# Expert products with w2 by one level of Strassen's algorithm in a graph and attention layer on one Trainium2 core

## The chip, the cores and the metric

The kernel runs on one core of one Trainium2 chip. The metric is the device time of one launch in microseconds; the kernel before takes 1625.79 us, the median of three runs (1625.36 to 1625.93). The profile is of one execution, whose span from the first to the last instruction is 1623.3 us.

## The reference

N = 4096 tokens of C = 256 channels pass a graph layer (a dense 4096x4096 adjacency times the features), causal attention with four heads, and a mixture of eight experts of which each token uses two. All arithmetic is fp32. The change is in the last part:

```python
flat = _rmsnorm(x, ln2_w).reshape(-1, Cx)
probs = jax.nn.softmax(flat @ router_w.T, axis=-1)
tp, ti = jax.lax.top_k(probs, TOPK)
...
for e in range(NE):
    hh = jax.nn.silu(flat @ w1[e].T) * (flat @ w3[e].T)
    out = out + weights[:, e:e + 1] * (hh @ w2[e].T)
return x + out.reshape(Bx, Tx, Cx)
```

The hidden size of an expert is 682: five chunks of 128 and a tail of 42.

## The kernel before

The program runs in three stages on the one core: the graph layer (to about 539 us), attention (its scores end at 1092 us) and the experts (hidden products from 1099 us to the end, the last steps of attention and routing among the first five turns). Instructions stand on each engine in the order in which the code emits them, so the order of the Python calls is the order of every engine's queue.

**Token groups.** For each expert, the routing stage has written the rows of its tokens (256 channels, the token's number, eight gate weights) into a list in DRAM. A group is 256 tokens of one expert (a whole group, two halves of 128) or 128 tokens (a small group). 42 groups are worked off in turns k = 0 to 41; the list `TURNS` gives the group of a turn. Turns 0 to 8 are whole groups; from 9 on whole and small ones mostly alternate (small at 9, 11, 13, 15, 16, 18, 20, 22, 24, 25, 27, 29, 31, 32, 34, 36 and 38), and turns 39, 40 and 41 are whole. 25 turns are whole and 17 small.

**A turn.** The loop over k emits: `hidden(k)`; the load of w1 and w3 for turn k + 3; `combine(k - 1)`; the load of the rows of turn k + 4; the load of w2 for turn k + 2. So the second products of a turn come after the first products of the next.

- `hidden(k)` (lines 1095 to 1126): for q = 0, 2, 4 a PSUM tile of two banks gets up to four 128-row blocks of w1 and w3 times the tokens (L1106); ScalarE takes silu of the w1 half (L1112); VectorE multiplies it with the w3 half into hT (L1113). The tail of 42 rows goes through L1121 and L1123 into a tile of its own. There are three such PSUM tiles in turn, two buffers for silu's output, and two each of hT and tail. After the first q the tokens of turn k + 1 are turned by TensorE (`prepare`, L1084: four 128x128 transposes for a whole group, two for a small one) in PSUM bank y, and two ScalarE operations (L1089) bring them into SBUF as xT.
- `combine(k)` (lines 1128 to 1178): VectorE picks the tokens' gate weights (pick L1135, gt L1139). For each half of 128 tokens six products of 256 columns (five chunks and the tail, L1151) accumulate in bank y. VectorE scales the sum by gt into y (L1162), and GpSimd adds y to the tokens' rows in DRAM by an indirect DMA (L1167, the put). The puts go to `acc_dram` up to turn 38. Then `acc_dram` is copied to `out` (L1268), and the puts of turns 39, 40 and 41 go to `out`. Turns 40 and 41 use bank ms for the first half and bank y for the second.

Banks y and ms are single buffers of 2 KB per partition. Weights lie in three rotating places cut out of two large tiles that earlier stages used (qT_all, res_all), so a product's name shows one of those as its source. All weight and row loads go through SyncE's one queue.

The graph stage already uses one level of Strassen's algorithm: lines 375 to 378 make sums of the adjacency, 400 to 403 those of the features, and lines 444 to 451 put seven products together.

Of the kernel before, what the change touches and what calls it, by code (L numbers as in the profile page):

```python
# [9 lines left out]
F32 = mybir.dt.float32  # L10
I32 = mybir.dt.int32
SP = mybir.EngineType.SP
AF = mybir.ActivationFunctionType
ALU = mybir.AluOpType
# [3 lines left out]
P = 128  # L18
N = 4096
C = 256  # L20
# [6 lines left out]
NF = 5  # L27
TAIL = HID - NF * P
T0 = 64
# [12 lines left out]
GR = 256  # L42
SM = 128
NA = -((NE * (GR - 1) - 2 * (N - 512)) // GR)
NW = -((NE * (GR - 1) - 2 * N) // GR)
# [8 lines left out]
NM = NG - RARE  # L54
# [12 lines left out]
def fast_kernel(  # L67
# [24 lines left out]
    nc = tc.nc  # L92
# [85 lines left out]
    kT = [kvp.tile([P, 512], F32, name=f"kT{b}") for b in range(NB)]  # L178
# [38 lines left out]
    with (  # L217
# [82 lines left out]
        T3 = G12  # L300
        HC = C // 2
# [230 lines left out]
    with (  # L532
# [259 lines left out]
                join(put, "late writes")  # L792


        def after(b):

            return [
                [None, lambda: inputs(b)],
                [None],
                [lambda: project(b, 0)],  # L800
                [lambda: project(b, 1)],
                [lambda: turn(b, 0)],
                [lambda: turn(b, 1), lambda: residual(b)],
                [lambda: logits(b)],
                [lambda: weigh(b)],
                [None, lambda: choose(b)],
                [None, lambda: scaled(b, 0)],
                [None, lambda: scaled(b, 1)],
                [lambda: place(b), lambda: scaled(b, 2)],
                [None, lambda: scaled(b, 3), lambda: scatter(b, 0, 0)],  # L810
                [None, lambda: scatter(b, 0, 1), lambda: scatter(b, 1, 0)],
                [None, lambda: scatter(b, 1, 1), lambda: scatter(b, 2, 0)],
                [None, lambda: scatter(b, 2, 1), lambda: scatter(b, 3, 0)],
                [None, lambda: scatter(b, 3, 1)],
            ]


        def last_qkv():
            b, made = NB - 1, {}

            def scales():
                stats(ax, b)
                var = mv[b][:, :, 1:2]
                power(rstd[b], var, 1.0, EPS_LN)
                power(both[b], var, *BOTH)

            def norm():
                made["h0"] = ax.tile([P, TB, ROW], F32, tag="row", name="h0_l")
                for t in range(TB):
                    normed(made["h0"][:, t, 0:C], b, t, both[b][:, t])  # L830

                made["hT"] = qT[b]

            def turned(h):
                tr = p_ms.tile([P, 2, 2, P], F32, tag="ms", name=f"tr_l{h}")
                for t in range(2):
                    for c in range(2):
                        nc.tensor.transpose(
                            tr[:, c, t, :], made["h0"][:, 2 * h + t, c * P : (c + 1) * P], ident
                        )  # L840
                for c in range(2):
                    nc.scalar.activation(
                        made["hT"][:, c, h * 2 * P : (h + 1) * 2 * P],
                        tr[:, c].rearrange("p t i -> p (t i)"),
                        AF.Copy, scale=ln1_sb[:, c : c + 1],
                    )

            def rotate(t):
                pj = p_ms.tile([P, 512], F32, tag="ms", name=f"pq_l{t}")
                room = ex.tile([P, NF, GR], F32, tag="hT", name=f"ro_l{t}")  # L850
                ro, r2 = (
                    room.rearrange("p k i -> p (k i)")[:, k : k + 384].rearrange(
                        "p (h s d) -> p h s d", s=2, d=HD // 2
                    )
                    for k in (0, 384)
                )
                rotated(ax, b, t, made["hT"], pj, ro, r2, cos_l[:, t, None, :], sin_l[:, t, None, :])
                made[t] = ro

            def turn_heads(t):  # L860
                tr = p_ms.tile([P, 2, 2, P], F32, tag="ms", name=f"trq_l{t}")
                heads(b, t, made.pop(t), tr)

            return [
                [None, scales], [None, norm], [lambda: turned(0)], [lambda: turned(1)],
                [lambda: rotate(0)], [lambda: rotate(1)],
                [lambda: turn_heads(0)], [lambda: rotate(2)],
                [lambda: turn_heads(1)], [lambda: rotate(3)],
                [lambda: turn_heads(2)], [lambda: turn_heads(3)],
                *guard(),  # L870
            ]
# [157 lines left out]
                join(put, "pads")  # L1029


        tails = [eg.tile([P, GR], F32, name=f"tail{n}") for n in range(2)]
        for t in tails:
            nc.gpsimd.memset(t, 0.0)

        at13 = (qT_all[:, 0 : 2 * W13], qT_all[:, 2 * W13 : 4 * W13], res_all[:, 0 : 2 * W13])
        W2 = (NF + 1) * C
        at2 = (
# [39 lines left out]
        def prepare(k, pool=p_y, tag="y"):  # L1078
# [13 lines left out]
                )  # L1092
            inputs_of[i] = xT

        def hidden(k, step=None, behind=None):
            i = TURNS[k]
            n = halves(i) * P
            w13_sb, xT = w13s[k % 3], inputs_of.pop(i)
            hT = ex.tile([P, NF, n], F32, tag="hT", name=f"hT_{i}")

            for q in range(0, NF + 1, 2):
                ps = next(p_sc).tile([P, 2, 2, GR], F32, tag="sc", name=f"h_{i}_{q}")
                ps = ps[:, :, :, 0:n]
                for m in range(2 * q, min(2 * q + 4, 2 * NF + 1)):
                    for c in range(2):
                        nc.tensor.matmul(  # L1106
                            ps[:, m % 2, m // 2 - q, :], w13_sb[:, c, m * P : (m + 1) * P],
                            xT[:, c, :], start=(c == 0), stop=(c == 1),
                        )
                both = 2 if q + 1 < NF else 1  # L1110
                si = ax.tile([P, 2, n], F32, tag="rden", name=f"si_{i}_{q}")
                nc.scalar.activation(si[:, 0:both, :], ps[:, 0, 0:both, :], AF.Silu)  # L1112
                nc.vector.tensor_mul(  # L1113
                    hT[:, q : q + both, :], si[:, 0:both, :], ps[:, 1, 0:both, :]
                )
                if q == 0 and behind is not None:
                    prepare(behind)
                if step and q < NF - 1:
                    step()

            nc.scalar.activation(si[T0 : T0 + TAIL, 1, :], ps[0:TAIL, 0, 1, :], AF.Silu)  # L1121
            tail = tails[k % 2][:, 0:n]
            nc.vector.tensor_mul(  # L1123
                tail[T0 : T0 + TAIL, :], si[T0 : T0 + TAIL, 1, :], ps[T0 : T0 + TAIL, 0, 1, :]
            )
            hidden_of[i] = (hT, tail)

        def combine(k):
            i = TURNS[k]
            n = halves(i)  # L1130
            w2_sb = w2s[k % 3]
            hT, tail = hidden_of.pop(i)
            r = rows.pop(i)
            pick = ex.tile([P, n, NE], F32, tag="pick", name=f"pick_{i}")
            nc.vector.tensor_mul(  # L1135
# [4 lines left out]
            y = ax.tile([P, HALF, C], F32, tag="yT1", name=f"y_{i}")  # L1140

            last = k >= NM - 2
            ps = [
                pool.tile([P, HALF, C], F32, tag=tag, name=f"ye_{i}_{tag}")
                for pool, tag in ((p_ms, "ms"), (p_y, "y"))[0 if last else 1 :]
            ]

            def products(h):
                cols = slice(h * P, (h + 1) * P)
                for q in range(NF + 1):  # L1150
                    nc.tensor.matmul(  # L1151
                        ps[h if last else 0][:, h, :],
                        hT[:, q, cols] if q < NF else tail[:, cols],
                        w2_sb[:, q, :], start=(q == 0), stop=(q == NF),
                    )

            for h in range(0 if last else n):
                products(h)
            for h in range(n):
                if last:  # L1160
                    products(h)
                nc.vector.tensor_scalar(  # L1162
                    y[:, h, :], ps[h if last else 0][:, h, :], gt[:, h], None, op0=ALU.mult
                )
                at = bass.IndirectOffsetOnAxis(ap=r[:, h, C : C + 1].bitcast(I32), axis=0)
                nc.gpsimd.memset(gap, 0.0)
                put = nc.gpsimd.indirect_dma_start(  # L1167
                    out=(acc_dram if k < NM - LAST else out)[:, :],
                    out_offset=at,
                    in_=y[:, h, :], in_offset=None, compute_op=ALU.add,  # L1170
                )
                if h:
                    free(put, f"half {i}", "an expert has a token once")
                else:
                    join(put, f"half {i}")
                if i < NA:
                    free(put, "last x", "the tokens of the first groups are others")
                    join(put, "first sums")
# [834 lines left out]
```

## Time and profile before

| what | from | value |
|---|---|---|
| median time | times | 1625.79 us |
| span of the profiled execution | page | 1623.3 us |
| granted TensorE clock, mean | cores | 0.998 |
| products with w2 in bank y (L1151) | tile | 780 records in 65 halves |
| transposes of tokens (L1084) | tile | 134 |
| hidden products (L1106) | page | 1848 records, 335 us busy |
| y scaled (L1162), 128x256 | page | 65, 481 ns each |
| puts to acc_dram and out (L1167) | page and groups | 67, 1.57 us of GpSimd each |
| w1 and w3 of a turn | DMA issues | 1408 KB, 7.6 to 8.0 us to landing |
| w2 of a turn | DMA issues | 768 KB, 5.0 to 5.3 us to landing |

How to read it: PE is TensorE's matmuls, PEld its weight loads, DVE is VectorE, ACT ScalarE, POOL GpSimd, SP SyncE. A timeline line gives the start, the duration, the engine, the code line, the operation, its output and inputs, the shape and how many instructions are merged; in brackets is the idle time before it and what ended it. Durations of matmuls overlap, as they are pipelined, so the distance of their starts is what one costs in a stream. A group's line gives total busy time and the mean of one in ns, then the idle time before.

### The profile page before, as it was taken

The numbers are of one execution on the slowest core, as the hardware profiler recorded it, in microseconds if no ns is written. First come the engines' busy times: TensorE is split into PE (matmuls) and PEld (weight loads), VectorE is DVE, ScalarE is ACT, GpSimd is POOL, SyncE is SP. The second block draws the span as 40 slices with busy tenths as digits, with TensorE's granted clock in tenths as the row PEclk, the third lists the DMA queues.
The fourth block names the chain that finished last, engine by engine and source line by source line (L and its number), as shares of the span: only waits on it lengthen the run. The fifth ranks groups of instructions, "written<-read, shape, count | busy, mean of one in ns | idle before, by whom it ended". The sixth has DMA issues, their size and how long they took to land.

```text
span 1623.3 us, 24752 instructions
## 1 busy us (share of the span) xinstructions
PE 1600.2 (99%) x9588; PEld 1156.7 (71%) x9588; DVE 930.4 (57%) x1914; ACT 457.1 (28%) x866; POOL 402.6 (25%) x604
## 2 busy tenths in 40 slices
PE   8999999999999999999999999999999999999997
PEld 5779999999999544343343433338888998999986
DVE  5656656656665678778878888793432222222222
ACT  2110100000000455554454554553211121221211
POOL 1001111112112220443334332322422222222122
PEclk9999999999999999999999999999999999999999
DMA  6224434433433000000101000067756777777765
GB/s 227 98 77 143 151 130 160 147 142 135 159 134 133 4 0 1 24 31 28 37 17 40 28 13 28 22 195 229 241 160 206 230 250 235 233 246 220 243 222 148
DMA packets 67711, 209.73 MB, mean 129 GB/s; under 512 B 14656, under 2 KB 46272, under 8 KB 53952
## 3 DMA queue, kind: packets, MB, share of 16 engines
q1 hardware_dynamic: 54592, 190.32, 33.7%
q0 software_dynamic: 12720, 17.47, 5.6%
q8 instruction: 78, 1.28, 0.3%
q14 instruction: 49, 0.40, 0.1%
q10 hardware_dynamic: 272, 0.26, 0.0%
HBM read 180.81 MB, written 31.42 MB: 131 GB/s over the span
## 4 chain that ended last, share of the span: by engine, by line
PE 91%; DVE 5%; ACT 2%; issue 1%; DMA 0%; POOL 0%; SPq 0%; DVEq 0%; POOLq 0%; ACTq 0%
PE acc L424 24%; PE h L1106 20%; PE ya L591 12%; PE sc L556 11%; PE ye_y L1151 10%; PE pf L386 3%; DVE sum L579 3%; PE pq L184 3%; PE po L625 2%; ACT pt L561 1%; PE tx L1084 1%; PE dn L604 1%; PE tr L319 1%; DVE rden L609 1%; PE trq L212 1%
## 5 line engine op out<-in xcount | busy, mean ns | idle before, releaser
L561 ACT ACTIVATE pt<-sc 128x1024 f32<-128x1024 f32 (+3 forms) x288 | 251.7, 958 | 201.4 <-PE sc L556 168.0
L579 DVE TENSOR_TENSOR sum<-sum,pt 128x1024 f32<-128x1024 f32 (+3 forms) x258 | 293.8, 1139 | 20.5 <-POOL pt L563 0.5
L424 PE MATMUL acc<-g,a 128*128 128x128 f32 x2048 | 255.7, 275 | 0.0
L556 PE MATMUL sc<-qT_all,kT 64*128 64x512 f32 (+3 forms) x1152 | 251.7, 570 | 3.0 <-ACT pt L561 2.2
L591 PE MATMUL ya<-pt,vv 128*64 128x512 f32 (+3 forms) x1152 | 242.6, 563 | 0.0
L424 PEld LDWEIGHTS acc<-g,a 128*128 128x128 f32 x2048 | 241.8, 192 | 0.0
L1106 PE MATMUL h<-xT,qT_all 128*128 128x256 f32 (+1 forms) x1232 | 220.5, 335 | 0.0
L1113 DVE TENSOR_TENSOR hT<-si,h 128x256 f32<-128x256 f32 (+2 forms) x126 | 64.1, 509 | 260.9 <-ACT si L1112 260.9
L1106 PEld LDWEIGHTS h<-xT,qT_all 128*128 128x128 f32 x1232 | 194.2, 191 | 18.9 <-issue 1.0
L556 PEld LDWEIGHTS sc<-qT_all,kT 64*128 64x128 f32 x1152 | 103.5, 186 | 138.8 <-issue 104.0
L591 PEld LDWEIGHTS ya<-pt,vv 128*64 128x64 f32 x1152 | 76.3, 136 | 145.4 <-issue 139.9
L1167 POOL DMA_INDIRECT acc_dram<-y,rows x61 | 96.1, 1575 | 332.2 <-DVE y L1162 327.8
L1112 ACT ACTIVATE si<-h 128x256 f32<-128x256 f32 (+2 forms) x126 | 57.2, 454 | 376.2 <-PE h L1106 371.0
L1106 PE MATMUL h<-xT,res_all 128*128 128x256 f32 (+1 forms) x616 | 114.6, 342 | 0.0
L1106 PEld LDWEIGHTS h<-xT,res_all 128*128 128x128 f32 x616 | 100.3, 191 | 10.2 <-issue 0.2
L424 PE MATMUL acc<-g,more_sums 128*128 128x129 f32 (+1 forms) x768 | 101.7, 275 | 0.6 <-DVE more_sums L377 0.6
L424 PEld LDWEIGHTS acc<-g,more_sums 128*128 128x128 f32 x768 | 94.6, 192 | 7.5 <-issue 7.5
L1151 PE MATMUL ye_y<-res_all,hT 128*128 128x256 f32 x430 | 99.8, 379 | 0.0
L783 POOL DMA_INDIRECT lists<-row,slots x64 | 69.0, 1077 | 114.8 <-issue 111.8
L1151 PEld LDWEIGHTS ye_y<-res_all,hT 128*128 128x128 f32 x430 | 80.9, 190 | 10.5
L1162 DVE TENSOR_SCALAR y<-ye_y,gt 128x256 f32<-128x256 f32 x65 | 29.3, 481 | 86.0 <-PE ye_y L1151 85.9
L424 PE MATMUL acc<-g,qT_all 128*128 128x128 f32 (+1 forms) x512 | 74.0, 274 | 0.0
(231 smaller groups left out, 1713.6 us busy)
## 6 DMA issues: line engine op xcount, KB each, us to landing
a<-in_adj_dram SPq DMA_DIRECT2D x64, 1024.0 KB, 4.7
qT_all<-in_w_dram SPq DMA_DIRECT2D x28, 1408.0 KB, 8.0
res_all<-in_w_dram SPq DMA_DIRECT2D x28, 768.0 KB, 5.3
res_all<-in_w_dram SPq DMA_DIRECT2D x14, 1408.0 KB, 7.6
qT_all<-in_w_dram SPq DMA_DIRECT2D x14, 768.0 KB, 5.0
rows<-lists SPq DMA_DIRECT2D x25, 265.0 KB, 2.8
lists<-pad SPq DMA_DIRECT2D x8, 662.5 KB, 13.9
res_all<-in_x_dram SPq DMA_DIRECT2D x8, 512.0 KB, 10.0
```

Source lines behind the costliest of these rows:

```text
L184: nc.tensor.matmul(pj, hT[:, c, t * P : (t + 1) * P], wqkv_sb[:, c, :], start=(c == 0), stop=(c == 1),)
L424: nc.tensor.matmul(acc[t][bank][:, at : at + w], m[left][:, k, t * P : (t + 1) * P], g[jb][:, right, k, 0:w], start=(jb == 0 and k == 0 an ...
L556: nc.tensor.matmul(ps[:, j, :w], kT[sb][hd, i * P : (i + 1) * P], qT[b][hd, p, off:], start=True, stop=True,)
L561: nc.scalar.activation(pt[:, :, :w], ps[:, :, :w], AF.Exp, scale=HD ** -0.5)
L579: nc.vector.tensor_add(sums[b, p][:, :, off:], before[:, :, off:], pt[:, :, : 512 - off])
L591: nc.tensor.matmul(accs[b, p][hd, off:], vv[sb][:, i, hd], pt[:, j, : 512 - off], start=(s == 0), stop=(s == TB * b + TB - 1),)
L783: put = nc.gpsimd.indirect_dma_start(out=lists[:, :], out_offset=bass.IndirectOffsetOnAxis(ap=chosen[b][:, k, t, :], axis=0), in_=flats[b] ...
L1106: nc.tensor.matmul(ps[:, m % 2, m // 2 - q, :], w13_sb[:, c, m * P : (m + 1) * P], xT[:, c, :], start=(c == 0), stop=(c == 1),)
L1112: nc.scalar.activation(si[:, 0:both, :], ps[:, 0, 0:both, :], AF.Silu)
L1113: nc.vector.tensor_mul(hT[:, q : q + both, :], si[:, 0:both, :], ps[:, 1, 0:both, :])
L1151: nc.tensor.matmul(ps[h if last else 0][:, h, :], hT[:, q, cols] if q < NF else tail[:, cols], w2_sb[:, q, :], start=(q == 0), stop=(q == NF),
L1167: put = nc.gpsimd.indirect_dma_start(out=(acc_dram if k < NM - LAST else out)[:, :], out_offset=at, in_=y[:, h, :], in_offset=None, comput ...
```

## The change

A product of a whole group is (256 tokens x 768) times (768 x 256), the 768 being five chunks, the tail and zeros around the tail. One level of Strassen's algorithm (in Winograd's form) cuts tokens, the inner dimension and the outputs in two each and makes seven products of halves in place of eight, at the price of sums before and after. It is done in 17 turns: 6, 7, 8, 10, 12, 14, 17, 19, 21, 23, 26, 28, 30, 33, 35, 37 and 39. It is for having fewer columns to stream through TensorE.

- The tail becomes the sixth chunk of hT, which is now two fixed tiles for even and odd turns. The rotation of the last block's heads borrows the same tiles.
- `split(k)` stands at the end of `hidden(k)`: eight VectorE operations of 128x384, four on the hidden values and four on w2. Sums go to buffers that attention has left (kT, vv), two sets for even and odd turns; S3 and T3 are written over their inputs.
- `seven_products(k)` stands in `combine(k)`: seven products of 128 columns, three chunks each; four in bank y and three in bank ms. Then one ScalarE copy and seven VectorE additions of 128x128 make the four quarters, and ScalarE scales the two halves into y in place of VectorE.
- From turn 6 on `prepare` of the next turn stands at the end of `hidden`, in bank ms, and no longer after the first q in bank y.

```diff
+        SEVEN = [k for k in range(6, NM - 2) if TURNS[k] < NW]
...
+            first = k % 2 * 3
+            for n, s in enumerate(("S1", "S2", "S4")):
+                m[s] = kT[first + n][:, 0 : 3 * P].rearrange("p (j i) -> p j i", j=3)
+            for n, s in enumerate(("T1", "T2", "T4")):
+                m[s] = vv[first + n][:, 0:3, :]
+            m["S3"], m["T3"] = m["A21"], m["G12"]
+            nc.vector.tensor_add(m["S1"], m["A21"], m["A22"])
+            nc.vector.tensor_sub(m["S2"], m["S1"], m["A11"])
+            nc.vector.tensor_sub(m["S4"], m["A12"], m["S2"])
+            nc.vector.tensor_sub(m["S3"], m["A11"], m["A21"])
+            nc.vector.tensor_sub(m["T1"], m["G12"], m["G11"])
+            nc.vector.tensor_sub(m["T3"], m["G22"], m["G12"])
+            nc.vector.tensor_sub(m["T2"], m["G22"], m["T1"])
+            nc.vector.tensor_sub(m["T4"], m["T2"], m["G21"])
...
+            for number, left, right in (
+                (1, "A11", "G11"), (2, "A12", "G21"), (6, "S2", "T2"), (7, "S3", "T3"),
+                (5, "S1", "T1"), (3, "S4", "G22"), (4, "A22", "T4"),
+            ):
+                n = len(p)
+                p[number] = banks[n // 4][:, n % 4, :]
+                for j in range(3):
+
+                    nc.tensor.matmul(
+                        p[number], m[left][:, j, :], m[right][:, j, :],
+                        start=(n % 4 == 0 and j == 0), stop=(j == 2), skip_group_check=True,
+                    )
...
+            nc.scalar.copy(u2, p[1])
+            nc.vector.tensor_add(c[0][:, 0], u2, p[2])
+            nc.vector.tensor_add(u2, u2, p[6])
+            nc.vector.tensor_add(u3, u2, p[7])
+            nc.vector.tensor_add(u4, u2, p[5])
+            nc.vector.tensor_add(c[0][:, 1], u4, p[3])
+            nc.vector.tensor_sub(c[1][:, 0], u3, p[4])
+            nc.vector.tensor_add(c[1][:, 1], u3, p[5])
...
-            hT = ex.tile([P, NF, n], F32, tag="hT", name=f"hT_{i}")
+            hT = hTs[k % 2][:, :, 0:n]
+            free_bank = k >= SEVEN[0]
...
-                if q == 0 and behind is not None:
+                if q == 0 and behind is not None and not free_bank:
                     prepare(behind)
...
+            if behind is not None and free_bank:
+                prepare(behind, p_ms, "ms")
+            hidden_of[i] = hT
+            if k in SEVEN:
+                split(k, hT)
...
+                if seven:
+                    nc.scalar.activation(
+                        y[:, h, :], done[h].rearrange("p h o -> p (h o)"), AF.Copy, scale=gt[:, h]
+                    )
+                else:
+                    nc.vector.tensor_scalar(
+                        y[:, h, :], ps[h if last else 0][:, h, :], gt[:, h], None, op0=ALU.mult
+                    )
```

More of the change, by code (lines that the diff above doesn't have):

```diff
@@ L792, in scatter @@
                 join(put, "late writes")
+        hTs = [eg.tile([P, NF + 1, GR], F32, name=f"hT{n}") for n in range(2)]
+        for t in hTs:
+            nc.gpsimd.memset(t[:, NF, :], 0.0)
         def after(b):
@@ L849, in rotate @@
                 pj = p_ms.tile([P, 512], F32, tag="ms", name=f"pq_l{t}")
-                room = ex.tile([P, NF, GR], F32, tag="hT", name=f"ro_l{t}")
+                room = hTs[t % 2]
                 ro, r2 = (
@@ L1029, in write_pads @@
                 join(put, "pads")
-        tails = [eg.tile([P, GR], F32, name=f"tail{n}") for n in range(2)]
-        for t in tails:
-            nc.gpsimd.memset(t, 0.0)
         at13 = (qT_all[:, 0 : 2 * W13], qT_all[:, 2 * W13 : 4 * W13], res_all[:, 0 : 2 * W13])
@@ L1093, in prepare, with split @@
             inputs_of[i] = xT
+        SEVEN = [k for k in range(6, NM - 2) if TURNS[k] < NW]
+        parts_of = {}
+        def split(k, hT):
+            w2_sb = w2s[k % 3]
+            m = {}
+            for c in range(2):
+                chunks = hT.rearrange("p (j c) i -> p c j i", c=2)[:, c]
+                weights = w2_sb.rearrange("p (j c) o -> p c j o", c=2)[:, c]
+                for h in range(2):
+                    m[f"A{h + 1}{c + 1}"] = chunks[:, :, h * P : (h + 1) * P]
+                    m[f"G{c + 1}{h + 1}"] = weights[:, :, h * P : (h + 1) * P]
+            first = k % 2 * 3
[12 more added lines that the diff above has]
+            nc.vector.tensor_sub(m["T4"], m["T2"], m["G21"])
+            parts_of[k] = m
@@ new lines, in seven_products @@
+        def seven_products(k):
+            i = TURNS[k]
+            m = parts_of.pop(k)
+            HC = C // 2
+            banks = [
+                pool.tile([P, 4, HC], F32, tag=tag, name=f"ye_{i}_{tag}")
+                for pool, tag in ((p_y, "y"), (p_ms, "ms"))
+            ]
+            p = {}
+            for number, left, right in (
[9 more added lines that the diff above has]
+                    )
+            c = [vv[6 + k % 2].rearrange("p (r h) o -> p r h o", r=2)[:, r] for r in range(2)]
+            u2 = u4 = c[0][:, 1]
+            u3 = c[1][:, 1]
+            nc.scalar.copy(u2, p[1])
[6 more added lines that the diff above has]
+            nc.vector.tensor_add(c[1][:, 1], u3, p[5])
+            return c
@@ L1121, in hidden @@
             nc.scalar.activation(si[T0 : T0 + TAIL, 1, :], ps[0:TAIL, 0, 1, :], AF.Silu)
-            tail = tails[k % 2][:, 0:n]
             nc.vector.tensor_mul(
-                tail[T0 : T0 + TAIL, :], si[T0 : T0 + TAIL, 1, :], ps[T0 : T0 + TAIL, 0, 1, :]
+                hT[T0 : T0 + TAIL, NF, :], si[T0 : T0 + TAIL, 1, :], ps[T0 : T0 + TAIL, 0, 1, :]
             )
-            hidden_of[i] = (hT, tail)
+            if behind is not None and free_bank:
[3 more added lines that the diff above has]
+                split(k, hT)
         def combine(k):
@@ L1131, in combine @@
             w2_sb = w2s[k % 3]
-            hT, tail = hidden_of.pop(i)
+            hT = hidden_of.pop(i)
             r = rows.pop(i)
@@ L1142, in combine @@
             last = k >= NM - 2
[L1143 to L1146, printed above, removed]
+            seven = k in SEVEN
+            if seven:
+                done = seven_products(k)
+            else:
+                ps = [
+                    pool.tile([P, HALF, C], F32, tag=tag, name=f"ye_{i}_{tag}")
+                    for pool, tag in ((p_ms, "ms"), (p_y, "y"))[0 if last else 1 :]
+                ]
             def products(h):
@@ L1152, in products @@
                         ps[h if last else 0][:, h, :],
-                        hT[:, q, cols] if q < NF else tail[:, cols],
-                        w2_sb[:, q, :], start=(q == 0), stop=(q == NF),
+                        hT[:, q, cols], w2_sb[:, q, :], start=(q == 0), stop=(q == NF),
                     )
-            for h in range(0 if last else n):
+            for h in range(0 if last or seven else n):
                 products(h)
@@ L1161, in combine @@
                     products(h)
-                nc.vector.tensor_scalar(
-                    y[:, h, :], ps[h if last else 0][:, h, :], gt[:, h], None, op0=ALU.mult
-                )
+                if seven:
+                    nc.scalar.activation(
+                        y[:, h, :], done[h].rearrange("p h o -> p (h o)"), AF.Copy, scale=gt[:, h]
+                    )
+                else:
+                    nc.vector.tensor_scalar(
+                        y[:, h, :], ps[h if last else 0][:, h, :], gt[:, h], None, op0=ALU.mult
+                    )
                 at = bass.IndirectOffsetOnAxis(ap=r[:, h, C : C + 1].bitcast(I32), axis=0)
```

## The prediction

> **What bounds the kernel now.** I read the page's busy shares first, then the table of stretches, then the timeline of one pair of expert turns, then the groups with shapes kept apart, then the timeline of the last 50 us.
>
> ```profile
> PE 1600.2 (99%) x9588; PEld 1156.7 (71%) x9588; DVE 930.4 (57%) x1914; ACT 457.1 (28%) x866; POOL 402.6 (25%) x604
> ```
>
> TensorE is busy through the span. The table of stretches says it for the expert stage alone: from 1114 to 1615 us TensorE 500.6 of 501.0 us, weight loads 450.5, VectorE 137.2, ScalarE 102.5, GpSimd 125.9, DMA share 0.71. So a product saved there is time saved, and VectorE has room on average. Two turns in the timeline, a whole group's w2 products (1264.52) and a small group's hidden ones (1306.85):
>
> ```profile
> 1264.52 2.32 PE L1151 MATMUL ye_y<-res_all,hT 128*128 128x256 f32 x10
> ...
> 1269.70 3.62 PE L1106 MATMUL h<-xT,qT_all 128*128 128x256 f32 x16
> ...
> 1306.85 3.29 PE L1106 MATMUL h<-xT,qT_all 128*128 128x128 f32 x28
> ...
> 1309.98 2.32 PE L1151 MATMUL ye_y<-res_all,hT 128*128 128x256 f32 x10
> ```
>
> Durations overlap, so the reader must take starts. 24 instructions lie between 1264.52 and 1269.70: 0.2158 us each for 256 columns. 28 lie between 1306.85 and 1309.98: 0.1118 us each for 128. One product in the code is two instructions (12 products of a whole group, 24 records).
>
> The end of the kernel is not bound by TensorE alone. Here is turn 39 (whole), from the end of its hidden products on, and the last puts:
>
> ```profile
> 1576.85 2.32 PE L1151 MATMUL ye_y<-res_all,hT 128*128 128x256 f32 x10
> 1577.05 0.38 ACT L1112 ACTIVATE si<-h 128x256 f32<-128x256 f32 x1 [1.99 <-PE h L1106]
> 1577.47 0.42 DVE L1113 TENSOR_TENSOR hT<-si,h 128x256 f32<-128x256 f32 x1 [1.69 <-ACT si L1112]
> 1577.92 0.38 ACT L1121 ACTIVATE si<-h 42x256 f32<-42x256 f32 x1 [0.49 <-DVE hT L1113]
> 1578.33 0.42 DVE L1123 TENSOR_TENSOR tail<-si,h 42x256 f32<-42x256 f32 x1 [0.44 <-ACT si L1121]
> ...
> 1579.65 0.48 DVE L1162 TENSOR_SCALAR y<-ye_y,gt 128x256 f32<-128x256 f32 x1 [0.49 <-PE ye_y L1151]
> ...
> 1580.41 1.57 POOL L1167 DMA_INDIRECT acc_dram<-y,rows  x1 [8.97 <-DVE y L1162]
> ...
> 1584.29 0.62 SPq L1268 DMA_DIRECT2D out_dram<-acc_dram  x1
> ...
> 1601.10 1.57 POOL L1167 DMA_INDIRECT out_dram<-y,rows  x1 [19.01 <-DMA out_dram<-acc_dram]
> ...
> 1602.98 1.57 POOL L1167 DMA_INDIRECT out_dram<-y,rows  x1 [0.19 <-DVE hT L1113]
> ...
> 1607.61 1.57 POOL L1167 DMA_INDIRECT out_dram<-y,rows  x1 [2.95 <-DVE y L1162]
> ...
> 1610.20 1.57 POOL L1167 DMA_INDIRECT out_dram<-y,rows  x1 [0.91 <-DVE gt L1139]
> ...
> 1612.03 0.48 DVE L1162 TENSOR_SCALAR y<-ye_ms,gt 128x256 f32<-128x256 f32 x1 [1.82 <-PE ye_ms L1151]
> ...
> 1615.18 1.57 POOL L1167 DMA_INDIRECT out_dram<-y,rows  x1 [3.30 <-DVE y L1162]
> ...
> 1617.06 1.57 POOL L1167 DMA_INDIRECT out_dram<-y,rows  x1 [0.19 <-issue]
> ```
>
> Turn 38's put (1580.41) releases the copy of acc_dram to out (1584.29); the copy holds turn 39's puts until 1601.10; and a group's puts wait for those of the group before on the same tensor. That last is my reading: y of turn 41 was done at 1612.5, its put went at 1615.18, 4.98 us after turn 40's second. The span ends at 1623.3, 6.24 us after the last put.
>
> [...]
>
> **The change part by part.** W is a whole turn (256 tokens), s a small one (128). 17 W turns, 6 to 39, get seven half-width products; T is the moment at which TensorE is through a W turn's hidden products and starts what follows (1576.85 above).
>
> *Products.* 24 x 0.2158 = 5.18 us go, 7 x 3 x 2 = 42 instructions at 0.1118 = 4.70 us come: 0.48 us saved each, 17 x 0.484 = **8.2 us**, all on the path.
>
> *Sums ahead (split).* Eight 128x384 VectorE operations. SBUF to SBUF is shown for 512 (0.684 to 0.692) and 256 elements (0.42), and 384 by another line:
>
> ```profile
> L376 DVE TENSOR_TENSOR qT_all<-qT_all,a 128x512 f32<-128x512 f32 x32 | 22.2, 692 | 5.8 <-PE acc L424 3.3
> L190 DVE TENSOR_TENSOR ro<-pq,cos 128x384 f32<-128x384 f32 x28 | 15.6, 558 | 62.4 <-ACT vv L188 62.4
> ```
>
> [...] I take 0.557 plus 0.035 between (1.1 us idle over 32 at the halving's third line): 4.7 us. Bounds: 0.55 to 0.69, the 512-element row. They begin when the tail is done, T+1.9, and end at T+6.6; queued behind are the preceding turn's pick, gt and y, then the next turn's hT.
>
> *Does TensorE wait?* Usual case: W, then s, with an s before. TensorE: two transposes 0.22, the preceding s turn's w2 products 12 x 0.2158 = 2.59, hidden products of s 44 x 0.1118 = 4.92, four transposes 0.44: T+8.2, where the seven products begin in bank y. That bank is free when y of the preceding turn is read: 6.6 + pick and gt 0.4 + y 0.48 = T+7.5. Slack 0.7 us (0.45 where another s follows and two transposes do). The first four products, 24 x 0.1118 = 2.68, end at T+10.9; then bank ms is needed, which the moved transposes fill. VectorE's hT of the s turn ends at 8.7, the tail's silu at 9.0, two xT copies of 0.47 at T+10.0. Slack 0.9. In a W turn not behind a split, tail silu ends at 1.45 after its hidden products and xT at 2.4, before the 0.44 + 2.68 on TensorE. So 0 us of waiting, but no more than 0.08 us per split operation is to spare. The 0.44 us of transposes only move.
>
> *Sums behind.* One ScalarE copy (0.27 to 0.31 at the GNN's like line), seven VectorE additions of 128x128 (0.28 to 0.29), two ScalarE scalings (near 0.42): some 3 us after the products, both banks free 1.5 us after them, beside hidden products of 9.5 us. Nothing. *One hT tile with the tail in it, rotation in it, a memset moved*: nothing, same operations and two buffers as before.
>
> *Loads.* The weights' queue waits for puts: the waits show 318 us in 38 waits of the row loads for puts. The preceding s turn's y comes at T+7.5 instead of T+3.3, so loads behind it are 4.2 us later. A w2 load issued at 1266.79 (lands in some 5.3) had its use at 1287.36; now split wants it at about 1281. Slack of 9 falls to about 5: nothing.
>
> *The end.* Turn 39 has a split too, so y of turn 38, its put and the copy come 4.2 us later: done at T+7.5 against 1580.13 - 1576.85 = 3.3. In old times: copy done 1605.3, turn 39's second put 1607.2, then 4.9 for landing, 1.9 for the second put, 4.98, 1.9, 6.24: end near 1627.1, or +3.8. The TensorE path (0.5 us shorter) no longer sets it. Sixteen of the seventeen groups save ahead of that point: 16 x 0.484 = 7.7.
>
> Sum: -7.7 + 3.8 = -3.9 to -4.0 us, **1621.8 us**.
>
> **The rivals.**
> - *The end catches up.* If turn 41's wait is for y after all, puts at 1605.3, 1607.2, 1609.1, 1610.9, 1612.8 fall behind y again and the end stays TensorE's: -8.2, 1617.6. For it: the record names VectorE as releaser at 1615.18. Against: y was done 2.7 us before.
> - *VectorE becomes the bound, slower than before.* If three-run operands or GpSimd's use of SBUF bring a split operation to 0.69 us, the chain is 1.06 us longer, 0.4 to 0.6 over the slack: 17 x 0.5 = 8.5 us back, and the end another 1 later: -4.0 + 8.5 + 1 = +5.5, 1631. Against: the operation on runs of 32 elements (L195, 192 elements, 0.348) pays nothing for its runs.
> - *The seven products don't reach 0.1118* (changes of operand every six instructions, semaphores): at 0.1155 each the saving is 0.33, 17 x 0.33 = 5.6, -5.3 + 3.8 = -1.5, 1624.3. Against: the GNN's stretch of the same kind runs 8 instructions from 299.73 to 300.63, 0.1125.
>
> **How the numbers follow.** Forecast 0.58, catching up 0.15, dearer products 0.13, VectorE 0.14. Within the forecast the landing (4 to 5 us twice) and the split (7.8 to 8.3 for y) move the end by 1.5 us. Range 1617.3 to 1626.5: it holds the first three cases and a VectorE chain that overruns by a tenth or two per group. The bound of 0.2% is 1622.5; about four fifths of the forecast and all of catching up lie under it: faster 0.64, same 0.20, slower 0.16.
>
> **What would show it.** Starts of the seven products 0.112 apart; VectorE near 231 us in the stage (137.2 + 17 x (8 x 0.557 + 7 x 0.287 - 2 x 0.48)) with split operations of 0.55 to 0.56; no idle TensorE ahead of the first and the fifth product; puts and copy of the end at some 22 us from copy's end to the span's end. Wrong if TensorE idles on y or xT in each pair, or if the last put follows y directly.

## The result and the profile after

The changed kernel takes 1620.81 us, the median of six runs (1618.56 to 1622.21), against 1625.28 us (1624.71 to 1625.93) for the kernel before beside it: a ratio of 0.9971, 95% interval 0.9958 to 0.9984, 2.6 to 6.8 us less. The forecast was 1621.8 us.

The busy line of the page, to be held against that of before:

```profile
PE 1592.0 (98%) x9894; PEld 1159.0 (72%) x9894; DVE 1014.8 (63%) x2135; ACT 480.9 (30%) x917; POOL 403.4 (25%) x604
```

There are 306 more TensorE instructions (17 turns x 18), 8 us less of TensorE's time and 84 us more of VectorE's. The table of stretches (columns: stretch, its length, then busy time and instructions of PE, PEld, DVE, ACT and POOL, the clock, the DMA share, GB/s) tells whether TensorE waits for that extra work in the middle of the stage:

```profile
1264.00:1414.00 150.00, 150.00 (x1021) 140.72 (x1021) 69.03 (x186) 40.18 (x102) 35.09 (x42) 1.00 0.75 237
1414.00:1564.00 150.00, 150.00 (x988) 139.82 (x987) 68.25 (x181) 39.97 (x101) 30.60 (x38) 1.00 0.75 237
```

It does not: 150 of 150 us, twice. Next comes one pair of turns in the timeline, a whole turn's split and the small turn behind it. TensorE was through the whole turn's hidden products at 1254.67, which is T of the forecast:

```profile
1254.67 0.38 PE L1085 MATMUL tx<-ident,rows 128*128 128x128 f32 x2
...
1254.89 2.76 PE L1228 MATMUL ye_y<-qT_all,hT 128*128 128x256 f32 x12
...
1256.61 0.56 DVE L1119 TENSOR_TENSOR kT<-hT 128x384 f32<-128x384 f32 x1
...
1260.39 0.56 DVE L1126 TENSOR_TENSOR vv<-vv,res_all 128x384 f32<-128x384 f32 x1
...
1260.86 0.16 DVE L1208 TENSOR_TENSOR pick<-rows,mine 128x8 f32<-128x8 f32 x1
...
1261.33 0.48 DVE L1243 TENSOR_SCALAR y<-ye_y,gt 128x256 f32<-128x256 f32 x1
...
1262.83 1.50 PE L1147 MATMUL ye_y<-res_all,hT 128*128 128x128 f32 x12
...
1263.52 0.84 ACT L1090 ACTIVATE xT<-tx,ln_sb 128x256 f32<-128x256 f32 x2
...
1265.51 0.83 PE L1147 MATMUL ye_ms<-vv,kT 128*128 128x128 f32 x6
...
1267.52 9.66 PE L1176 MATMUL h<-xT,qT_all 128*128 128x256 f32 x44
```

Two margins can be read from it. The preceding turn's y, which empties bank y, ends at 1261.81 and the seven products begin at 1262.83: about 1.0 us. xT, which empties bank ms, ends at 1264.36 and the fifth product begins at 1265.51: 1.15 us. The 42 instructions lie between 1262.83 and 1267.52, 0.1117 us each.

The end of the changed kernel (timeline, from T of turn 39 on):

```profile
1568.35 0.60 PE L1085 MATMUL tx<-ident,rows 128*128 128x128 f32 x4
1568.38 1.57 POOL L1248 DMA_INDIRECT acc_dram<-y,rows  x1 [0.19 <-issue]
...
1574.99 0.48 DVE L1243 TENSOR_SCALAR y<-ye_y,gt 128x256 f32<-128x256 f32 x1
...
1579.95 1.57 POOL L1248 DMA_INDIRECT acc_dram<-y,rows  x1 [9.89 <-DVE hT L1183]
...
1583.70 0.62 SPq L1349 DMA_DIRECT2D out_dram<-acc_dram  x1
...
1599.62 1.57 POOL L1248 DMA_INDIRECT out_dram<-y,rows  x1 [17.98 <-DMA out_dram<-acc_dram]
...
1601.49 1.57 POOL L1248 DMA_INDIRECT out_dram<-y,rows  x1 [0.19 <-ACTq L2015]
...
1606.21 1.57 POOL L1248 DMA_INDIRECT out_dram<-y,rows  x1 [3.04 <-DVE y L1243]
...
1612.66 1.57 POOL L1248 DMA_INDIRECT out_dram<-y,rows  x1 [2.89 <-DMA out_dram<-y,rows]
...
1614.54 1.57 POOL L1248 DMA_INDIRECT out_dram<-y,rows  x1 [0.19 <-issue]
```

y of turn 38 is done at 1575.47, 7.12 us after T (3.28 before). But its put goes only at 1579.95, 4.48 us after y, where before it followed y by 0.28 us. The releaser named there, an hT of turn 40, has nothing to do with the put: it is merely what ended last beside it. The span ends at 1620.5, 5.96 us after the last put. So in this execution, the slowest of the six, the end has lost twice: once by y, and once by something that the forecast did not have.

Executions of one kernel differ by 1 to 2 us that arise ahead of the expert stage: the first hidden product started between 1098.5 and 1100.6 in the traces below. Each trace is therefore cut in two: **stage**, from the first hidden product to T of turn 39, and **end**, from there to the span's end. The column ratio has the timed runs against the kernel before that ran beside them.

| kernel | median us | ratio (95% interval) | stage us | end us |
|---|---|---|---|---|
| before | 1625.28 | | 478.13 | 46.45 |
| changed | 1620.81 | 0.9971 (0.9958 to 0.9984) | 469.85 | 52.15 |
| e6_turned_only | 1626.16 | 0.9999 (0.9991 to 1.0007) | 477.69 | 47.4 |
| e5_sums_only | 1627.88 | 1.0009 (1.0 to 1.0017) | 477.69 | 48.2 |
| e8_two_more | 1625.10 | 0.9991 (0.9983 to 1.0) | 473.47 | 50.45 |
| e7_four_more | 1642.92 | 1.0102 (1.0086 to 1.0117) | 490.09 | 51.0 |
| e1_no39 | 1619.04 | 0.995 (0.9937 to 0.9964) | 469.85 | 48.5 |
| e2_rows9 | 1621.64 | 0.9965 (0.9951 to 0.9978) | 469.85 | 49.4 |
| e4_before_rows9 | 1626.88 | 1.0002 (0.9994 to 1.001) | 478.13 | 46.85 |
| e3_rows9_late | 1618.06 | 0.9948 (0.9934 to 0.9961) | 469.85 | 46.7 |

The kernel before and e4_before_rows9 have 0.44 us of transposes in their stage that the others have in their end. Stage and end come from one execution each. Beside the eight experiments the kernel before took 1626.4 us, 1.1 us more than beside the changed kernel: so the experiments' times are compared by their ratio, or by their distance from the kernel before of the same session, and not as they stand.

### The profile page after: what moved, and what is told of

Same layout as the page of the kernel before. It is cut to its first block, busy times and chain, and to the rows that moved or that the text cites. A ratio compares the mean times of both kernels' runs of the same rounds, so it can differ in the third digit from the quotient of the medians.

```text
span 1620.5 us, 25640 instructions
## 1 busy us (share of the span) xinstructions
PE 1592.0 (98%) x9894; PEld 1159.0 (72%) x9894; DVE 1014.8 (63%) x2135; ACT 480.9 (30%) x917; POOL 403.4 (25%) x604
## 5 line engine op out<-in xcount | busy, mean ns | idle before, releaser
L1176 PE MATMUL h<-xT,qT_all 128*128 128x256 f32 (+1 forms) x1232 | 216.6, 335 | 0.0
L1176 PEld LDWEIGHTS h<-xT,res_all 128*128 128x128 f32 x616 | 99.9, 191 | 10.2 <-issue 0.2
L424 PEld LDWEIGHTS acc<-g,qT_all 128*128 128x128 f32 x512 | 66.5, 192 | 7.2 <-issue 7.2
L198 POOL TENSOR_TENSOR ro<-ro,r 128x192 f32<-128x192 f32 x28 | 16.5, 588 | 218.7 <-DVE r L195 218.7
L563 POOL TENSOR_SCALAR_AFFINE_SELECT pt<-pt 128x256 f32<-128x256 f32 x64 | 39.1, 634 | 127.7 <-ACT pt L561 126.9
```

What stands on the lines that cost most here:

```text
L198: nc.gpsimd.tensor_sub(ro[:, :, 0, :], ro[:, :, 0, :], r2[:, :, 0, :])
L424: nc.tensor.matmul(acc[t][bank][:, at : at + w], m[left][:, k, t * P : (t + 1) * P], g[jb][:, right, k, 0:w], start=(jb == 0 and k == 0 an ...
L563: nc.gpsimd.affine_select(out=pt[:, :, 0:P], in_=pt[:, :, 0:P], pattern=[[0, 2], [1, P]], compare_op=ALU.is_ge, fill=0.0, base=0, channel_ ...
L1176: nc.tensor.matmul(ps[:, m % 2, m // 2 - q, :], w13_sb[:, c, m * P : (m + 1) * P], xT[:, c, :], start=(c == 0), stop=(c == 1),)
```

## The experiments

Two questions stood open: are the stage's three parts (products, sums, turning) each worth what the forecast gave them, and what delays the end. For the end there were two theories. **A**, the forecast's: turn 39's split holds y of turn 38 on VectorE. **B**: the put of turn 38 waits for the put of turn 37 to land (landing is the completion that the trace records), and that put lands late because it lies beside weight loads. The loads and puts would then form a loop with a pace of its own (a put lands, its rows' buffer comes free, rows and weights are loaded, and the next put lands beside them), so that TensorE, 8 us ahead by then, meets the loads later in its own time. The last row load is issued at 1564.10 before and at 1565.89 after, although T of turn 39 is 8.5 us earlier. The traces' records of DMA completion speak for theory B: in the changed kernel turn 37's second put landed 10.85 us after it went, and turn 38's went 0.72 us behind that landing. So did the first put of each of nine groups in a row, from 1487.79 to 1579.95. In the kernel before turn 37's second put landed in 6.99 us, 3.66 us ahead of turn 38's put, which waited for y.

**The turning alone.** Transposes at the end of `hidden` in bank ms from turn 6 on; no split, no seven products.

```diff
-        SEVEN = [k for k in range(6, NM - 2) if TURNS[k] < NW]
+        SEVEN = [6]
...
-            if k in SEVEN:
-                split(k, hT)
...
-            seven = k in SEVEN
+            seven = False
```

> Only the turning of the next group's tokens stands at the end of a group's hidden products in bank ms from turn 6 on; the products are the old ones and no sums are made. Theory (the transposes only move, the copies to xT stay ahead of their use): before's time within 0.5 us. Rival (it frees bank y earlier and is itself worth something, or the later xT holds TensorE): 2 us or more either way.

Measured: 0.9999, and a stage of 477.69 us, which is that of before less the 0.44 us that moved. The theory held. The next experiment is held against this kernel, and not against before.

**The sums ahead alone.** Split in all 17 turns, S3 and T3 in spare buffers so that their inputs stay whole, products and scaling the old ones.

```diff
-            m["S3"], m["T3"] = m["A21"], m["G12"]
+            m["S3"], m["T3"] = (kT[n][:, 0 : 3 * P].rearrange("p (j i) -> p j i", j=3) for n in (6, 7))
...
-            seven = k in SEVEN
+            seven = False
```

> The sums ahead are made in all 17 turns as in the changed kernel, but nothing uses them: the products are the old twelve of 256 columns per whole group, with VectorE's scaling, so nothing is saved on TensorE. Theory of hidden sums (the slack of some 1 us in each pair holds): TensorE's stage is as long as before, only the end is later, since y of turn 38 comes 4 us later and its put waits for landing besides: 4 to 7 us over before, 1629 to 1632. Rival (the sums cost TensorE time in each turn, and the products save more than 0.48 each): TensorE idles in the pairs, 10 us or more over before, 1636.

Measured: the stage is 477.69 us, the same to the hundredth as without the sums, though VectorE is busy for 122.9 us in place of 76.2 of 300. The same stretch of e5_sums_only, then of e6_turned_only:

```profile
1264.00:1564.00 300.00, 300.00 (x1759) 273.67 (x1759) 122.91 (x304) 63.35 (x165) 67.05 (x80) 1.00 0.75 239
```

```profile
1264.00:1564.00 300.00, 300.00 (x1754) 273.52 (x1753) 76.17 (x206) 64.04 (x166) 65.76 (x78) 1.00 0.75 237
```

So the sums cost TensorE nothing, and the 7.84 us between 477.69 and 469.85 are the products of the 16 groups ahead of T of turn 39: 0.490 each. The whole time missed its expectation: 1.5 us over before, not 4 to 7. The put of turn 38 follows y at once here:

```profile
1584.79 0.48 DVE L1243 TENSOR_SCALAR y<-ye_y,gt 128x256 f32<-128x256 f32 x1
...
1585.55 1.57 POOL L1248 DMA_INDIRECT acc_dram<-y,rows  x1 [12.25 <-DVE y L1243]
```

That is T + 7.00 for y's end (1578.27 is T), and no wait for a landing. The first put behind the copy came 2.86 us later after T than in e6_turned_only (27.33 against 24.47), the end only 0.8 us: in e6_turned_only the puts of turn 40 wait for their y once more (13.0 us from turn 39's second put to turn 41's first, against 11.0 in e5_sums_only), and a late copy uses up that pause.

**How near VectorE is to the bound.** Four or two further additions at the end of each split.

```diff
+            spare = kT[6][:, 0 : 3 * P].rearrange("p (j i) -> p j i", j=3)
+            for n in range(4):
+                nc.vector.tensor_add(spare, m["S1"], m["S2"])
```

> The changed kernel with four further VectorE additions of 128x384 at the end of each split, 2.2 us more per turn, whose result nothing uses. Theory (a slack of 1.0 us in each pair of a small and a whole turn, as the changed kernel's trace has it): the 13 pairs in the middle overrun by 2.2 - 1.0 = 1.2 us each, TensorE idles ahead of the first of the seven products: +15 to 16 us, 1636 to 1637. Rival (no slack left: all 2.2 us cost): +29, 1650. Rival (VectorE far from the bound): no change, 1621.

> The same with two further additions, 1.1 us more per turn. Theory of a slack of 1.0 us: just used up, 0 to 0.3 us of idle TensorE per pair, 0 to 4 us over the changed kernel, 1621 to 1625. Rival (the slack is the forecast's 0.7 us and less): 0.4 to 0.65 us in each of 13 pairs, 5 to 8.5 us, 1626 to 1629.

With two, the stage grows by 3.6 us over the changed kernel's, inside the expectation; with four, by 20.2 us, more than the 15 to 16 expected. The waits of TensorE with four (total, how many, longest):

```profile
PE ye_y L1150 <- DVE y L1246: 15.4, 13, 1.3
PE tx L1085 <- DVE vv L1164: 1.1, 1, 1.1
```

Thirteen pairs, as counted, and the releaser is y, as the theory has it. With two, y ends just as the products want to begin (timeline of e8_two_more):

```profile
1263.64 0.48 DVE L1246 TENSOR_SCALAR y<-ye_y,gt 128x256 f32<-128x256 f32 x1
...
1264.18 1.60 PE L1150 MATMUL ye_y<-res_all,hT 128*128 128x128 f32 x12
```

T is 1255.91 there: y ends at T + 8.21, 1.07 us later than without the two, and the products begin 0.06 us behind it, at T + 8.27 instead of T + 8.16. The slack was thus 0.96 us. What the expectation for four left out: three of the 13 pairs have a small turn next, whose two transposes give 0.22 us less room; the first twelve instructions of the products take 1.44 us after a wait and 1.34 without one; and turning once waited 1.1 us for bank ms. 10 x (1.29 + 0.10) + 3 x (1.49 + 0.10) + 1.1 = 19.8, where 1.29 and 1.49 us are how much later the products began in these pairs.

**Turn 39 as before.** The last split and the last seven products undone.

```diff
-        SEVEN = [k for k in range(6, NM - 2) if TURNS[k] < NW]
+        SEVEN = [k for k in range(6, NM - 3) if TURNS[k] < NW]
```

> Turn 39 keeps its twelve products of full width; sixteen turns get seven. Theory A (the forecast's): what is lost at the end is y of turn 38 waiting behind the split of turn 39. Without that split the put of turn 38 goes some 3.6 us after the hidden products of turn 39, as before, and the copy and last puts come with TensorE: 1625.3 - 16 x 0.484 = 1617.5 us, 3.3 under the changed kernel. Theory B (a loop of puts and loads): the put of turn 38 waits for the landing of turn 37's second put (1568.38, free at 1579.9 in the changed kernel's trace, though y was done at 1575.5), which shares the DMA engines with weight loads; the row loads of all turns were issued at nearly the same absolute times in both traces (1564.1 and 1565.9 for the last), so this loop keeps its own pace. Then the put of turn 38 still goes near 1580 and the time stays within 0.7 us of the changed kernel, about 1620.5.

Theory A gave 1617.5 and B about 1620.5, both counted from a kernel before of 1625.3: 7.8 and 4.8 us less than before. Measured: 0.995, which is 8.1 us less than before (5.9 to 10.2), or 7.4 us by the medians. The timed runs go with A, and B lies outside the interval. The trace shows more (turn 37's second put, T of turn 39, y and put of turn 38):

```profile
1566.71 1.57 POOL L1248 DMA_INDIRECT acc_dram<-y,rows  x1 [0.19 <-issue]
...
1570.20 0.60 PE L1085 MATMUL tx<-ident,rows 128*128 128x128 f32 x4
...
1573.43 0.48 DVE L1243 TENSOR_SCALAR y<-ye_y,gt 128x256 f32<-128x256 f32 x1 [0.94 <-PE ye_y L1228]
...
1578.45 1.57 POOL L1248 DMA_INDIRECT acc_dram<-y,rows  x1 [10.06 <-DVE hT L1183]
```

y of turn 38 ends at T + 3.7, as A has it, but its put goes at T + 8.25, 4.5 us behind y, as B has it: turn 37's second put had landed only 11.0 us after it went (11.74 us lie between the two puts, 0.72 of them behind the landing). This execution was the slowest of its five (1620.51). How long the landing holds the put also differs between executions. Up to turn 39's split this is the program of the changed kernel, and yet turn 37's second put went at T - 3.5 here and at T + 0.03 there. Had the changed kernel's y, done at T + 7.1, met a put that is free at T + 8.25, the hold would have been 0.9 us and not 4.2.

**The loads freed of the puts.** From turn 6 on the rows go to nine buffers that attention has left, not five, so that row loads no longer wait for puts, and the loads come sooner.

```diff
-            r = ex.tile([P, HALF, ROW], F32, tag="rows", name=f"rows_{i}", bufs=5)
+            if k < 6:
+                r = ex.tile([P, HALF, ROW], F32, tag="rows", name=f"rows_{i}", bufs=5)
+            else:
+                r = sp.tile([P, 2, 512], F32, tag="pt", name=f"rows_{i}")[:, :, 0:ROW]
```

> The changed kernel, but from turn 6 on the rows lie in the nine buffers that attention's probabilities have left, in place of five, so that a row load does not wait for the last put. Theory A: buffers of rows play no part, the same as the changed kernel, 1620.8. Theory B: weight loads are issued when TensorE frees their places and not when a put lands, puts land sooner after their issue, and the put of turn 38 goes with y (1575.8 in place of 1580.0 in the trace): 4 us faster than the changed kernel, about 1616.7; what is left at the end is the split's 4.2 us.

The put moved as B said (timeline of e2_rows9: turn 37's second put, then y and put of turn 38):

```profile
1566.88 1.57 POOL L1251 DMA_INDIRECT acc_dram<-y,rows  x1 [0.19 <-issue]
...
1577.11 0.48 DVE L1246 TENSOR_SCALAR y<-ye_y,gt 128x256 f32<-128x256 f32 x1
...
1577.87 1.57 POOL L1251 DMA_INDIRECT acc_dram<-y,rows  x1 [9.30 <-DVE y L1246]
```

0.28 us behind y again. Two things made room. Turn 37's second put went 3.6 us ahead of T (1570.47) and not at T, and it landed after 3.85 us and not after 10.85. A wait for a landing did not go everywhere: turn 37's first put still went 0.72 us behind the landing of turn 36's. How busy the DMA engines were beside the second put is in the last two columns of the stretches (DMA share and GB/s), of the changed kernel first, then of e2_rows9:

```profile
1569.00:1572.00 3.00, 3.00 (x15) 2.65 (x14) 2.46 (x6) 1.21 (x3) 1.06 (x2) 1.00 0.98 356
1572.00:1575.00 3.00, 3.00 (x15) 2.64 (x15) 2.80 (x9) 0.00 (x0) 0.00 (x0) 1.00 1.00 331
```

```profile
1569.00:1572.00 3.00, 3.00 (x18) 2.64 (x17) 0.93 (x3) 0.82 (x3) 0.00 (x0) 1.00 0.45 49
1572.00:1575.00 3.00, 3.00 (x15) 2.65 (x14) 2.90 (x6) 0.78 (x2) 0.00 (x0) 1.00 0.00 0
```

Three weight loads were issued at 1566.52, 1567.42 and 1567.99 in the changed kernel, just ahead of the put at 1568.38. From there to the put's landing at 1579.23 the packets of the loads' queue took 71.0% of the 16 DMA engines' time, and those of the puts' queue 16.0%. Turn 37's second put took 10.85 us beside the three loads, whereas turn 38's, with the engines nearly idle ahead of it (a DMA share of 0.04 from 1578 to 1581) and no other queue's packets beside it until it landed, took 3.73 us and let the copy go 3.75 us after it. In what order the engines took the packets of the two queues is not shown. In time the change was far from B's 4 us: 0.9965 against 0.9971, some 1 us (0.3 by the medians' distance from before), and within the intervals. In the traces the end is 2.7 us shorter, but the changed kernel's trace is its slowest execution. A's delay was still there.

> The kernel before with nine row buffers from turn 6 on. Theory B: in the kernel before the put of turn 38 went 0.28 us after its y, so the loop had slack of its own and TensorE had no idle time: no change, 1625.3 within 0.6. A rival, that the row loads' waits cost the kernel before something too: faster by more than 1 us.

This is the control, the same edit of the rows in the kernel before: no change (1.0002). There the put followed y anyway.

**Both delays taken away.** e2_rows9, and turn 39's split after `combine(38)`, so that y of turn 38 stands ahead of it.

```diff
-            if k in SEVEN:
+            if k in SEVEN and k != 39:
                 split(k, hT)
...
+                if k == 39:
+                    split(k, hidden_of[TURNS[k]])
```

> As e2_rows9, and the split of turn 39 stands behind the scaling of turn 38's y on VectorE. Theory B with A: the put of turn 38 goes 3.6 us after the hidden products of turn 39, the copy ends with some 10 us to spare, and the end is TensorE's again: its last y (1606.5 in the changed trace) plus the 8.7 us of before, 1615.2 span: 5.4 us under the changed kernel, about 1615.5. Theory A alone: 1617. If neither holds: 1620.8.

Measured: 1618.06 us, 0.9948, which is 8.5 us less than before (6.3 to 10.7), the best of all. The expectations, 1615.5 with A and B and 1617 with A alone, are 9.8 and 8.3 us less than before, so the timed runs do not tell these two apart. The end is 46.7 us, no longer than e6_turned_only's 47.4, and its lines lie as before (T is 1569.43):

```profile
1573.42 1.63 POOL L1251 DMA_INDIRECT acc_dram<-y,rows  x1 [6.24 <-DVE y L1246]
...
1577.30 0.61 SPq L1354 DMA_DIRECT2D out_dram<-acc_dram  x1
...
1608.34 1.57 POOL L1251 DMA_INDIRECT out_dram<-y,rows  x1 [3.93 <-DVE y L1246]
```

The put is at T + 3.99, the copy at T + 7.87; turn 37's second put (1565.49) had landed in 3.8 us. So the forecast's 8.2 us were to be had from the products, and the end had taken the rest.

## Why the prediction was right, and where it was not

- **Products**: right. 0.1117 us per instruction, 7.84 us for the 16 groups ahead of T of turn 39, where the forecast had 7.7. Dearer products are ruled out.
- **Split**: the operations took 0.550 to 0.558 us (means by line), as said, and as the 0.558 of L190's 128x384 operation in the kernel before had it. But the eight took only 4.34 us, not 4.7, because some of them start before the one ahead has ended (0.47 us apart, see the last section). So y came at T + 7.14, not T + 7.5, and the slack was 0.96 us, not 0.7: 0.12 us per operation. VectorE's busy time in the stage (222 us against the forecast's 231) is less for the same reason, as the page counts overlap once. The longest of the 136 operations took 0.560 us, also among the two that ran beside a GpSimd instruction, so the 0.69 of the VectorE rival did not come. VectorE as the bound was two operations away: e8_two_more already waits, e7_four_more loses 20 us.
- **Work queued behind the split**: right. That what stands behind the split on VectorE waits for it was the forecast's assumption. The changed kernel's timeline shows it: the products that y reads were through at 1257.65, but pick, the first step towards y, started at 1260.86, 0.47 us behind the start of the split's last operation (1260.39).
- **xT and bank ms**: right, 1.15 us of slack where 0.9 was forecast. **Turning and sums behind**: nothing, shown by e6_turned_only for the one, and by the unbroken TensorE of the changed kernel for the other.
- **Loads**: here the forecast left something out. "Slack of 9 falls to about 5: nothing" asked only whether TensorE would wait for weights, and in the stage it never did. It did not ask what the loads do to the puts: turn 37's second put landed beside three loads and held turn 38's by 4.2 us in the profiled run. In the timed runs this is worth about 1 us or less (e2_rows9 against the changed kernel) and is not clear of the intervals.
- **The end**: right in its cause, y of turn 38 behind the split. y was later by 3.84 us (4.2 forecast), and the chain from the copy's end to the span's end was 20.9 us (21.8 forecast). Without turn 39's split the timed runs gain 3.4 us (0.9950 against 0.9971; 2.9 by the medians) although turn 39's 0.49 us are given up: 3.4 to 3.9 us for a forecast of 3.8. With the landing out of the way y is worth 2.7 us in the traces and 2.8 to 3.6 in the timed runs (e2_rows9 less e3_rows9_late, whose times do not overlap). With the old products it is worth less, 0.8 us in the traces and some 1.6 in the timed runs (e5_sums_only less e6_turned_only). That the sum came within 1 us is in part luck: delay and chain were each forecast somewhat too long, and the landing was left out.
- **Catching up** was wrong: turn 41's first put waited for a landing (1612.66, 6.6 us behind its y), as the forecast read it. In before it was so too, since turn 40's second put had landed at 1614.44 and turn 41's first went at 1615.18. But turn 40's puts there waited for y, and a late copy uses up that wait first: the chain from the copy's end was 22.2 us in before and 20.9 us in the changed kernel, where the forecast had taken off only 0.4 us.
- **Left open**: how often, and for how long, the landing holds the put. The two traces that show it were the slowest executions of their kernels (1622.21 and 1620.51 us), so the timed medians may have less of it.

## What to carry to other kernels

Work that is hidden behind TensorE turn by turn still delays what stands behind it on its own engine (here y of turn 38, by 3.84 us); look for the one turn whose output opens a serial tail (here a put that releases a copy), and put the extra work behind that output there. When TensorE gets faster but the loads keep their own pace, transfers can come to lie beside each other in another way (here a put landed 10.85 us after it went, and 6.99 us in the kernel before): check the puts as well as the loads' users. A single trace can show a delay larger than it is in most executions, so compare it with the timed runs before giving it a price. And when the kernel that is compared against drifts by a microsecond between sessions, compare differences from it and not bare times.

## What the runs showed of the hardware

- VectorE operations of 128x384, of 0.55 to 0.56 us each, started 0.58 to 0.60 us apart in the changed kernel's 17 splits where the second reads the sum that the one ahead wrote (S1 to S2, S2 to S4, T2 to T4) or overwrites what it read (T1 to T3). They started 0.46 to 0.48 us apart where neither holds (S4 to S3, S3 to T1, T3 to T2), but for one S3 to T1 of 1.05 us with a wait for w2. T3 written over its input started 0.59 us behind the operation ahead of it (1258.74, 1259.33), in its own buffer 0.47 us (e5_sums_only: 1582.34, 1582.81).
- An indirect accumulating put of 128 rows landed after 3.7 to 3.9 us with the DMA engines nearly idle (turn 38's: 3.73 in the changed kernel, 3.86 in before; DMA share 0.04 and 0.00 from 1578 to 1581), and after up to 11.0 us beside weight loads (10.85 in the changed kernel, 11.02 in e1_no39).
- A put that waited for the landing of the one before it went 0.72 us behind that landing, nine times in a row in the changed kernel.
